# One quarter of a recurrent step as bf16 matmuls on three-part operands: the parts made on GpSimd, their rows summed on VectorE

## The chip, the cores and the metric

The kernel runs on one core of one Trainium2 chip. The core's engines each have a queue of their own and meet through semaphores: TensorE (PE; its weight loads are listed as PEld), VectorE (DVE), ScalarE (ACT), GpSimd (POOL) and SyncE (SP, which issues the transfers here). SBUF is the working memory; PSUM takes the matmuls' results, in banks. The metric is the device time of one execution in microseconds (us), the median of some runs.

## What is computed

A gated recurrent network with 512 units runs over 512 time steps for a batch of 8, and its states are added to the input:

```
def step(h, x_t):
    fused = sigmoid(concat([x_t, h]) @ w_W + w_b)
    hidden_state, output_state = split(fused, 2)
    memory_state = x_t @ wx_W + wx_b + hidden_state * (h @ wh_W + wh_b)
    h_new = output_state * h + (1.0 - output_state) * tanh(memory_state)
    return h_new, h_new
out = x + states
```

Below, r is the sum behind `hidden_state`, z the sum behind `output_state`, and h (as a bank's column) the sum `h @ wh_W + wh_b`. All tensors are float32. The parts that hang on x alone can be computed ahead; the three products of the state with 512x512 weights cannot, since each step needs the state of the step before.

## The kernel before

**Layout.** The 512 units are split over 128 partitions and 4 chunks, and the chunks into half A (chunks 0 and 1) and half B (2 and 3). For a step, PE multiplies the state (the stationary operand, 128 rows by 32 columns, of which only the 8 columns of this step are not zero) with weights (the moving operand). The output goes to four column tiles j of 32 partitions each. Four steps make a group: each has its own 8 of the 32 rows in a bank, so one bank serves four steps, and the x part of the sums is put there ahead.

**Banks of a step.** Bank A (192 columns, weights `wa`) holds h, z and r of half A; bank B (128 columns of `wb`) r and h of half B; and bank C, 64 columns of the PSUM tile `cs` (the other 64 of `wb`), z of half B. `ORDER` (line 26) is the order of a step on PE: `A0 B0 A1 A2 A3 B1 B2 B3 C0 C1 C2 C3`, where the digit is the chunk k of the state that is multiplied. A0, B0 and A1 need only half A of the new state, A2 is the first to need half B. Each entry is four matmuls (one for each j). A float32 matmul shows as two weight loads and two matmuls in the trace.

**Work on x.** Behind C3 stand the matmuls of `x_step` (lines 528-538), which prepare the x part of later groups. `SHARE` (line 48) deals them out: 384 columns a step in the first four steps of eight, 288 in the last four. There are none in steps 0 to 4, less towards the end, and none in the last five steps.

**Behind the matmuls.** Once bank A is done, DVE transposes r, h and z of half A (`turn_r`, `turn_h`, `turn_z`), so that units stand on partitions; ACT takes the sigmoids; DVE's scan `memory(hf, q)` forms the argument of tanh, ACT the tanh, and the scan `update(hf, q)` the new state, for one chunk q of half hf at a time. In DVE's queue half B's transposes stand around the first update of half A, then come half B's `memory` and `update` scans. ACT copies the new state to another slot, then does the group work: copies into banks (`spread`) and the moves of x sums. POOL adds the states to x for the output (`add`), two additions a step, and makes four x sums in eight steps (`x_sum`).

**Order.** All instructions are recorded in the order of the program and emitted engine by engine; `Flow.plan` (lines 132-214) finds the waits from what each instruction reads and writes. In PSUM any access to a bank waits for the latest access of any other engine to it. The emitting code has one line for all instructions, so every row of the profile reads L227; rows are told apart by their tiles.

Of the kernel before, what the change touches and what calls it, by code (L numbers as in the profile page):

```python
# [18 lines left out]
B = 8  # L19
# [3 lines left out]

DVE_FILL = 23
IDLE = 3
# [3 lines left out]

BANKS = {"A": 192, "B": 128, "C": 64}  # L30

# [55 lines left out]
class Flow:  # L87
# [44 lines left out]
    def plan(self):  # L132
# [9 lines left out]
        for i, item in enumerate(self.items):  # L142
# [71 lines left out]
            done.append(snap)  # L214

    def emit(self, tc):

# [21 lines left out]
def tile_cond_rnn_residual(  # L239
# [115 lines left out]
    NH = 2 * GS  # L355
    hT = [[pair(n, f"hT{n}{i}", 32, 3) for i in range(NH)] for n in "AB"]

# [13 lines left out]
    nc.scalar.activation(const.tile([P, 1], F32, name="table"), zeros[:, :1], AF.Sigmoid)  # L371
    for n, t_ in enumerate(hd0[0] + hd0[1] + md0[0] + md0[1] + hT[0] + hT[1]):
        (nc.vector if n < DVE_FILL else nc.gpsimd).memset(t_, 0.0)
    for t_ in hd0[0] + hd0[1]:
        nc.gpsimd.memset(t_[:, :, :, 1], -1.0)
# [10 lines left out]
    def state(hf, i, slot=2):  # L386
# [7 lines left out]
        {"A": wide[q]["A"][:, : BANKS["A"]],  # L394
         "B": wide[q]["B"][:, : BANKS["B"]],
         "C": cs[:, HU * q : HU * q + HU]}
        for q in range(2)
    ]
    xps = [psum.tile([P, 512], F32, name=f"xp{q}") for q in range(2)]
    piece = psum.tile([P, 512], F32, name="eps")  # L400
    eps = piece[HI, :W]

    def mm(out_, lhsT, rhs, start=False):
# [44 lines left out]
    def spread(g, names):  # L448

        for n in names:  # L450
            nc.scalar.copy(banks[g % 2][n], source(g)[:, XP[n]])

    def turn_x(g, hf):
# [101 lines left out]
    keep(0)  # L555
    spread(0, "ABC")
    for hf in range(2):
# [7 lines left out]
    for i in range(T):  # L565
# [8 lines left out]
        for n in (ORDER if i else FIRST).split():  # L574
            if n == "x":
                take(first[3], 1)
                continue
            bank, k = n[0], int(n[1])
            hs = hT[k // 2][i % NH][:, :, k % 2, 2]
            for j in range(NQ):  # L580
                mm(ps[bank][32 * j : 32 * j + 32, :], hs, wh(bank, k, j))
        if T - 17 <= i < T - 5:
# [6 lines left out]
        def scan(c_, out_, d0, d1):  # L589
# [10 lines left out]
            "h": (pa[:, :HU], ps["B"][:, HU:]),  # L600
            "z": (pa[:, HU : 2 * HU], ps["C"]),
            "r": (pa[:, 2 * HU :], ps["B"][:, :HU]),
# [25 lines left out]
        def turn_z(hf):  # L628
            tz, _ = turned("z", hf)
            if hf == 0:  # L630
# [32 lines left out]
        turn_h(1)  # L663
        update(0, 0)
        turn_z(1)
        nc.after(update(0, 1), r_done[1])
        if i == T - 1:
# [5 lines left out]
            )  # L673
        memory(1, 0)
        memory(1, 1)
        update(1, 0)
        update(1, 1)
        for hf in range(2):
            act(state(hf, i + 1, 0), state(hf, i + 1), AF.Copy)
        if i < 3:  # L680
            inst = load_x(i + 1)
            if i == 0:
                nc.after(inst, r_done[1])
# [6 lines left out]
        if o == LAST:  # L690
            if u == 2:
                spread(2 * o + 1, "AB")
                turn_x(2 * o + 1, 0)
                turn_x(2 * o + 1, 1)
            elif u == 3:
                spread(2 * o + 1, "C")
        elif u == 0:
            if o == 0:
                spread(1, "A")
            if sums:  # L700
                nc.scalar.copy(reg(BE), reg(AL))
# [4 lines left out]
        elif u == 1:  # L706
            if sums:
                nc.scalar.copy(more[HI], eps)
            spread(2 * o + 1, "BC" if o == 0 else "AC")
        elif u == 2:  # L710
# [3 lines left out]
            if o:  # L714
                spread(2 * o + 1, "B")
        elif u == 3:
            if sums:
# [132 lines left out]
```

## Time and profile before

| | us |
|---|---|
| median of 3 runs (lowest, highest) | 1654.64 (1654.48, 1655.43) |
| the profiled execution | 1657.46 |
| its span in the trace | 1655.7 |
| granted TensorE clock, mean | 0.999 |
| POOL busy | 301.9 |
| transfers, mean rate | 19 GB/s |

The span runs from the first to the last instruction of the program; 1.8 us of the profiled execution lie outside of it. A row of groups gives engine, operation, tiles (out<-in, without buffer numbers), shapes and count, then the busy time in us, the mean of one in ns, and the idle time of the engine before them with what ended it. A row of the timeline gives the start in us, how long the (merged) instructions took together in us, engine, line, operation, tiles, shapes and count; the brackets hold idle time before it and who ended that. Ends of matmuls are modelled, and include the way through the array, so that the distance of two starts says more than a duration.

### The profile page before, as it was taken

The numbers are of one execution on the slowest core, as the hardware profiler recorded it, in microseconds if no ns is written. First come the engines' busy times: TensorE is split into PE (matmuls) and PEld (weight loads), VectorE is DVE, ScalarE is ACT, GpSimd is POOL, SyncE is SP. The second block draws the span as 40 slices with busy tenths as digits, with TensorE's granted clock in tenths as the row PEclk, the third lists the DMA queues.
The fourth block names the chain that finished last, engine by engine and source line by source line (L and its number), as shares of the span: only waits on it lengthen the run. The fifth ranks groups of instructions, "written<-read, shape, count | busy, mean of one in ns | idle before, by whom it ended". The sixth has DMA issues, their size and how long they took to land.

```text
span 1655.7 us, 125580 instructions
## 1 busy us (share of the span) xinstructions
PE 1645.6 (99%) x54298; PEld 1500.2 (91%) x54298; DVE 1153.9 (70%) x9194; ACT 1193.8 (72%) x5998; POOL 301.9 (18%) x1279
## 2 busy tenths in 40 slices
PE   9999999999999999999999999999999999999998
PEld 5999999999999999999999999999999999999987
DVE  6776676676766766767667767677676766766765
ACT  3777777777777777777777777777777777777775
POOL 1211111111111111111111111111111111111111
PEclk9999999999999999999999999999999999999999
DMA  4000000000000000000000000000000000000000
GB/s 182 11 18 14 15 15 16 16 14 15 16 15 15 14 16 16 14 14 15 16 15 14 14 17 14 15 14 17 14 14 15 17 14 14 15 17 10 10 10 10
DMA packets 37284, 31.14 MB, mean 19 GB/s; under 512 B 4084, under 2 KB 35060, under 8 KB 36600
## 3 DMA queue, kind: packets, MB, share of 16 engines
q1 hardware_dynamic: 36576, 22.89, 4.5%
q8 instruction: 424, 6.95, 1.7%
q14 instruction: 132, 1.08, 0.2%
q10 hardware_dynamic: 152, 0.22, 0.1%
HBM read 14.70 MB, written 8.39 MB: 14 GB/s over the span
## 4 chain that ended last, share of the span: by engine, by line
PE 99%; DVE 1%; issue 0%; ACT 0%; DVEq 0%; SPq 0%
PE A L227 40%; PE B L227 26%; PE xp L227 18%; PE cs L227 13%; PE eps L227 1%; DVE tr L227 0%; DVE m L227 0%; DVE tz L227 0%; DVE md1B L227 0%; DVE md1A L227 0%; DVE hTA L227 0%; DVE hTB L227 0%; ACT hTB L227 0%; DVE zeros L227 0%; DVE rows L227 0%
## 5 line engine op out<-in xcount | busy, mean ns | idle before, releaser
L227 PE MATMUL A<-wa,hTA 128*32 128x192 f32 x8192 | 559.5, 326 | 2.4 <-DVE hTA L227 2.2
L227 PE MATMUL B<-wb,hTA 128*32 128x128 f32 x8192 | 454.8, 273 | 0.0
L227 PE MATMUL A<-wa,hTB 128*32 128x192 f32 x8192 | 448.6, 326 | 0.0
L227 PEld LDWEIGHTS A<-wa,hTA 128*32 128x32 f32 x8192 | 292.5, 122 | 124.6 <-DVE hTA L227 101.7
L227 DVE STREAM_TRANSPOSE tr<-A 128x64 f32<-128x64 f32 x512 | 128.0, 250 | 367.6 <-PE A L227 367.6
L227 POOL TENSOR_TENSOR ot<-xin,hTB 128x16 f32<-128x16 f32 x495 | 123.8, 250 | 1290.4 <-DVE hTB L227 1290.4
L227 PEld LDWEIGHTS B<-wb,hTA 128*32 128x32 f32 x8192 | 352.6, 122 | 2.8 <-issue 0.3
L227 PE MATMUL B<-wb,hTB 128*32 128x128 f32 x8192 | 339.6, 273 | 0.0
L227 PEld LDWEIGHTS A<-wa,hTB 128*32 128x32 f32 x8192 | 330.4, 122 | 9.1 <-DVE hTB L227 0.2
L227 ACT ACTIVATE md0A<-tr 128x16 f32<-128x16 f32 x512 | 112.4, 219 | 238.5 <-DVE tr L227 238.4
L227 PE MATMUL xp<-tw,sx 128*32 128x384 f32 (+2 forms) x1464 | 269.7, 433 | 0.0
L227 PEld LDWEIGHTS B<-wb,hTB 128*32 128x32 f32 x8192 | 262.3, 122 | 0.2 <-issue 0.2
L227 PE MATMUL cs<-wb,hTB 128*32 128x64 f32 x8192 | 230.3, 219 | 0.4 <-issue 0.3
L227 PE MATMUL cs<-wb,hTA 128*32 128x64 f32 x8192 | 230.2, 219 | 0.0
L227 DVE TENSOR_TENSOR_SCAN hTB<-hd0B,hTB 128x24 f32<-128x24 f32 x1024 | 158.0, 196 | 99.8 <-ACT hTB L227 99.8
L227 PE MATMUL xp<-wx,xin 128*32 128x384 f32 (+4 forms) x1348 | 219.1, 413 | 0.0
L227 PEld LDWEIGHTS cs<-wb,hTA 128*32 128x32 f32 x8192 | 207.5, 122 | 0.0
L227 DVE TENSOR_TENSOR_SCAN hTA<-hd0A,hTA 128x24 f32<-128x24 f32 x1024 | 190.9, 186 | 0.0
L227 ACT ACTIVATE hd0B<-tz 128x16 f32<-128x16 f32 x512 | 115.6, 226 | 94.5 <-DVE tz L227 94.5
L227 PEld LDWEIGHTS cs<-wb,hTB 128*32 128x32 f32 x8192 | 180.2, 122 | 0.7 <-issue 0.7
L227 ACT ACTIVATE hTB<-hTB 128x16 f32<-128x16 f32 x512 | 120.3, 235 | 79.1 <-DVE hTB L227 72.8
L227 ACT ACTIVATE hTA<-m 128x8 f32<-128x8 f32 x1024 | 160.8, 206 | 0.6 <-DVE m L227 0.3
(101 smaller groups left out, 2680.6 us busy)
## 6 DMA issues: line engine op xcount, KB each, us to landing
out_dram<-ot SPq DMA_DIRECT2D x128, 64.0 KB, 1.6
xin<-in_x_dram SPq DMA_DIRECT2D x112, 64.0 KB, 2.4
wx<-in_wx_dram SPq DMA_DIRECT2D x4, 768.0 KB, 7.0
wa<-in_wa_dram SPq DMA_DIRECT2D x4, 384.0 KB, 9.8
wb<-in_wb_dram SPq DMA_DIRECT2D x1, 1152.0 KB, 13.7
xin<-in_x_dram SPq DMA_DIRECT2D x3, 256.0 KB, 3.7
wb<-in_wb_dram SPq DMA_DIRECT2D x1, 384.0 KB, 14.1
head<-in_xh_dram ACTq DMA_DIRECT2D x1, 208.0 KB, 4.7
```

What stands on the lines that cost most here:

```text
L227: inst = getattr(self, item.op, getattr(engine, item.op, None))(*item.args, **item.kw)
```

## The change

z of half B (bank C) is no longer multiplied in float32. From step 3 on, h and the weights of bank C are each split into three bf16 parts that add up to the float32 number. The three parts of the 8 batch columns stand side by side as one stationary operand of 24 columns (`split`), loaded once for each k and j; three bf16 matmuls of 64 columns follow, one for each part of the weights (`wb` itself, of which the upper halves are read at every second bf16 element, `w2` and `w3`). The second and third are `kept`: they use the loaded operand again and have no weight load. Steps 0 to 2 stay float32.

- PE: an entry of C has 4 weight loads and 12 matmuls in place of 8 and 8.
- POOL makes the parts: two instructions for each half of the state, four in each step, ahead of the two additions; `w2` and `w3` once, at the end of step 0.
- The three parts come out in three groups of 8 rows, so the 32 rows of `cs` no longer serve four steps: each step has its own 64 columns, eight steps fill the tile. The x part is put into each step's columns by an ACT instruction with a mask (`spread_c`), zero but in 8 of the 32 rows: eight such instructions in eight steps in place of two copies.
- DVE sums the four groups of rows with a `tensor_reduce` behind the transpose. In half B the order on DVE becomes transpose, `memory(1, 0)`, the sum, `update(0, 1)`, `memory(1, 1)`, and on ACT the first tanh of half B comes ahead of the sigmoid of z.
- The states lie in one tile of both halves per ring place (`hs`, shown as hT), twice as wide as the data, the upper half zero. The start's fills are dealt out anew between DVE and POOL.

```diff
-DVE_FILL = 23
+DVE_FILL = 14
...
-BANKS = {"A": 192, "B": 128, "C": 64}
+BANKS = {"A": 192, "B": 128}
+PLAIN = 3
...
+    def kept(self, out, lhsT, rhs):
+        t = self.nc.tensor
+        return t.add_instruction(
+            mybir.InstMatmult(
+                name=self.nc.get_next_instruction_name(),
+                ins=[t.lower_ap(rhs), t.lower_ap(lhsT)],
+                outs=[t.lower_ap(out)],
+                start_tensor_calc=False,
+                stop_tensor_calc=False,
+                tile_size=(128, 32),
+                tile_position=(0, out.offset // 512 // 32 * 32),
+                bass_skip_group_check=True,
+                ldweights=False,
+                engine=mybir.EngineType.PE,
+            )
+        )
...
-    hT = [[pair(n, f"hT{n}{i}", 32, 3) for i in range(NH)] for n in "AB"]
+    hs = [const.tile([P, NQ, 64, 3], F32, name=f"hT{i}") for i in range(NH)]
+    hT = [[t_[:, 2 * n : 2 * n + 2, :32].rearrange("p c n s -> p n c s") for t_ in hs] for n in range(2)]
+    split = [const.tile([P, NQ, 3, B], F32, name=f"split{i}") for i in range(2)]
+    w2 = const.tile([P, NQ, NQ, HU], F32, name="w2")
+    w3 = const.tile([P, NQ, NQ, HU], F32, name="w3")
+    mask = const.tile([P, GS, 32], F32, name="mask")
...
-    for n, t_ in enumerate(hd0[0] + hd0[1] + md0[0] + md0[1] + hT[0] + hT[1]):
+    for n, t_ in enumerate(hd0[0] + hd0[1] + md0[0] + md0[1] + hs):
         (nc.vector if n < DVE_FILL else nc.gpsimd).memset(t_, 0.0)
+    steps = const.tile([P, GS, 32], F32, name="steps")
+    nc.vector.memset(steps, 0.0)
+    for n in range(GS):
+        nc.vector.memset(steps[:, n, B * n : B * n + B], 1.0)
+    nc.vector.transpose(mask.rearrange("p s n -> p (s n)"), steps.rearrange("p s n -> p (s n)"))
...
+    def high(t_):
+        return t_.bitcast(BF16)
+    def parts(out_, i, k, j):
+        lhsT = high(split[i % 2])[:, k].rearrange("p u b -> p (u b)")[:, 1::2]
+        for n, t_ in enumerate((wb[:, k, j, :HU], w2[:, k, j], w3[:, k, j])):
+            (nc.tensor.kept if n else mm)(out_, lhsT, high(t_)[:, 1::2])
...
+    def cell(i):
+        return cs[:, HU * (i % NH) : HU * (i % NH) + HU]
+
+    def spread_c(g, steps_):
+
+        for s in steps_:
+            nc.scalar.activation(
+                cell(GS * g + s), source(g)[:, XP["C"]], AF.Copy, scale=mask[:, s, :1]
+            )
...
-            hs = hT[k // 2][i % NH][:, :, k % 2, 2]
+            lhsT = hs[i % NH][:, k, :32, 2]
             for j in range(NQ):
-                mm(ps[bank][32 * j : 32 * j + 32, :], hs, wh(bank, k, j))
+                if bank == "C" and i >= PLAIN:
+                    parts(cell(i)[32 * j : 32 * j + 24], i, k, j)
+                else:
+                    to = cell(i) if bank == "C" else ps[bank]
+                    mm(to[32 * j : 32 * j + 32, :], lhsT, wh(bank, k, j))
...
-            tz, _ = turned("z", hf)
+            if hf:
+                t_, tz = tzb, tz_sum
+                nc.vector.tensor_reduce(
+                    tz, t_.rearrange("p c (u b) -> p c b u", u=4), mybir.AxisListType.X, ALU.add
+                )
+            else:
+                tz, _ = turned("z", hf)
...
+        tzb = work.tile([P, 2, 32], F32, tag="tzB", name=f"tzB_{i}")
+        tz_sum = work.tile([P, 2, B], F32, tag="tzs", name=f"tzs_{i}")
+        nc.vector.transpose(tzb.rearrange("p c n -> p (c n)"), raw["z"][1])
+        memory(1, 0)
         turn_z(1)
-        nc.after(update(0, 1), r_done[1])
+        update(0, 1)
...
-        memory(1, 0)
         memory(1, 1)
...
+            if PLAIN <= i + 1 < T:
+                ks, s1 = slice(2 * hf, 2 * hf + 2), B * ((i + 1) % GS)
+                t_, new = split[(i + 1) % 2][:, ks], hs[(i + 1) % NH][:, ks]
+                nc.gpsimd.tensor_tensor(
+                    t_[:, :, :2].rearrange("p k u b -> p k b u"),
+                    new[:, :, s1 : s1 + B, 2].unsqueeze(3).broadcast_to([P, 2, B, 2]),
+                    high(new).rearrange("p k (u n) s -> p k n u s", u=2)[:, :, s1 : s1 + B, :, 5],
+                    ALU.subtract,
+                )
+                nc.gpsimd.tensor_tensor(t_[:, :, 2], t_[:, :, 0], high(t_)[:, :, 0, 1::2], ALU.subtract)
+        if i == 0:
+            for to, t_ in ((w2, wb[:, :, :, :HU]), (w3, w2)):
+                nc.gpsimd.tensor_tensor(to, t_, high(t_)[:, :, :, 1::2], ALU.subtract)
...
-                spread(2 * o + 1, "C")
+                spread_c(2 * o + 1, (0, 1))
+            elif u == 4:
+                spread_c(2 * o + 1, (2, 3))
+            elif u < 2:
+                spread_c(2 * o, (2 + u,))
...
+                spread_c(2 * o, (2,))
...
-            spread(2 * o + 1, "BC" if o == 0 else "AC")
+            spread(2 * o + 1, "B" if o == 0 else "A")
+            if o:
+                spread_c(2 * o, (3,))
+            spread_c(2 * o + 1, (1,) if o else (0, 1))
...
+            spread_c(2 * o + 1, (2, 3))
...
+            spread_c(2 * o + 2, (0,))
...
-            spread(2 * o + 2, "C")
+            spread_c(2 * o + 2, (1,))
+            if o + 1 < LAST:
+                spread_c(2 * o + 3, (0,))
```

How this stands on the engines is shown at three places, each in a step with x work in the middle of the program. On PE, before, the end of a step (A, B and cs are the banks, hTA and hTB the halves of the state, the xp rows are x work):

```order
L227 MATMUL A_118<-wa,hTB_76 32x192 x8
L227 MATMUL B_119<-wb,hTA_68 32x128 x4
L227 MATMUL B_119<-wb,hTB_76 32x128 x8
L227 MATMUL cs<-wb,hTA_68 32x64 x8
L227 MATMUL cs<-wb,hTB_76 32x64 x8
L227 MATMUL xp_122<-wx,xin_133 32x384 x2
```

And with the change, from the last of bank B to the third pair of k and j (w_77 and w_78 are `w2` and `w3`, split_75 the parts of the state):

```order
L247 MATMUL B_117<-wb,hT_67 32x128 x12
L247 MATMUL cs<-wb,split_75 24x64
L221 MATMUL cs<-w_77,split_75 24x64
L221 MATMUL cs<-w_78,split_75 24x64
L247 MATMUL cs<-wb,split_75 24x64
L221 MATMUL cs<-w_77,split_75 24x64
L221 MATMUL cs<-w_78,split_75 24x64
L247 MATMUL cs<-wb,split_75 24x64
```

The 16 float32 matmuls of C became 48 in bf16, three for each pair; what stands ahead and behind is as before.

On DVE, before, from half B's transposes of r and h to the end of a step (tr and md1B are these, hTA and hTB are `update`, m is `memory`, tz<-cs the transpose of z of half B; the scans are listed here as SCALAR_TENSOR_TENSOR):

```order
L227 STREAM_TRANSPOSE tr_1_138<-B_119 128x64
L227 STREAM_TRANSPOSE md1B_89<-B_119 128x64
L227 SCALAR_TENSOR_TENSOR hTA_69<-hd0A_92,hTA_68 128x24
L227 STREAM_TRANSPOSE tz_1_139<-cs 128x64
L227 SCALAR_TENSOR_TENSOR hTA_69<-hd0A_92,hTA_68 128x24
L227 SCALAR_TENSOR_TENSOR m_1_135<-md0B_85,md1B_89 128x16 x2
L227 SCALAR_TENSOR_TENSOR hTB_77<-hd0B_94,hTB_76 128x24 x2
```

With the change (tzB is the transpose, tzs the sum over the row groups):

```order
L247 STREAM_TRANSPOSE tr_1_137<-B_119 128x64
L247 STREAM_TRANSPOSE md1B_87<-B_119 128x64
L247 SCALAR_TENSOR_TENSOR hT_73<-hd0A_89,hT_72 128x24
L247 STREAM_TRANSPOSE tzB_138<-cs 128x64
L247 SCALAR_TENSOR_TENSOR m_1_134<-md0B_83,md1B_87 128x16
L247 TENSOR_REDUCE tzs_139<-tzB_138 128x16
L247 SCALAR_TENSOR_TENSOR hT_73<-hd0A_89,hT_72 128x24
L247 SCALAR_TENSOR_TENSOR m_1_134<-md0B_83,md1B_87 128x16
L247 SCALAR_TENSOR_TENSOR hT_73<-hd0B_91,hT_72 128x24 x2
```

The first `memory` scan of half B moved ahead of the second update of half A, and the sum came between them. The first update of half A stays where it was.

On POOL, before, two steps (ot are the output additions, sx an x sum):

```order
L227 TENSOR_TENSOR ot_156<-xin_140,hTB_79 128x8x2
L227 TENSOR_TENSOR ot_156<-xin_140,hTA_71 128x8x2
L227 TENSOR_TENSOR sx_105<-xin_147 128x64
L227 TENSOR_TENSOR ot_156<-xin_140,hTB_80 128x8x2
L227 TENSOR_TENSOR ot_156<-xin_140,hTA_72 128x8x2
```

With the change, one step:

```order
L247 TENSOR_TENSOR split_76<-hT_72 128x2x8x2
L247 TENSOR_TENSOR split_76<-split_76 128x2x8
L247 TENSOR_TENSOR split_76<-hT_72 128x2x8x2
L247 TENSOR_TENSOR split_76<-split_76 128x2x8
L247 TENSOR_TENSOR sx_103<-xin_148 128x64
L247 TENSOR_TENSOR ot_124<-xin_140,hT_72 128x8x2 x2
```

The first pair of splits is that of half A and waits for its second update alone; the second pair waits for half B, as the output additions behind it did before.

More of the change, by code (lines that the diff above doesn't have):

```diff
@@ L394, in tile_cond_rnn_residual @@
         {"A": wide[q]["A"][:, : BANKS["A"]],
-         "B": wide[q]["B"][:, : BANKS["B"]],
-         "C": cs[:, HU * q : HU * q + HU]}
+         "B": wide[q]["B"][:, : BANKS["B"]]}
         for q in range(2)
@@ L555, in tile_cond_rnn_residual @@
     keep(0)
-    spread(0, "ABC")
+    spread(0, "AB")
+    spread_c(0, range(GS))
     for hf in range(2):
@@ L600, in tile_cond_rnn_residual @@
             "h": (pa[:, :HU], ps["B"][:, HU:]),
-            "z": (pa[:, HU : 2 * HU], ps["C"]),
+            "z": (pa[:, HU : 2 * HU], cell(i)),
             "r": (pa[:, 2 * HU :], ps["B"][:, :HU]),
@@ L699, in tile_cond_rnn_residual @@
                 spread(1, "A")
+            else:
+                spread_c(2 * o, (2,))
             if sums:
```

## The prediction

> **What bounds the kernel now.** I read the page first, then the timeline of PE alone, for the distance from step to step.
>
> ```profile
> PE 1645.6 (99%) x54298; PEld 1500.2 (91%) x54298; DVE 1153.9 (70%) x9194; ACT 1193.8 (72%) x5998; POOL 301.9 (18%) x1279
> ...
> PE 99%; DVE 1%; issue 0%; ACT 0%; DVEq 0%; SPq 0%
> ```
>
> PE is busy throughout and makes up the chain that ended last. But ends of matmuls are modelled, so this alone doesn't say how far the recurrence is from binding. The first matmuls of five steps in the middle say more:
>
> ```profile
> 800.25 0.55 PE L227 MATMUL A<-wa,hTA 128*32 128x192 f32 x8
> ...
> 803.36 0.55 PE L227 MATMUL A<-wa,hTA 128*32 128x192 f32 x8
> ...
> 819.40 0.59 PE L227 MATMUL A<-wa,hTA 128*32 128x192 f32 x8
> ...
> 822.67 0.59 PE L227 MATMUL A<-wa,hTA 128*32 128x192 f32 x8
> ...
> 825.77 0.53 PE L227 MATMUL A<-wa,hTA 128*32 128x192 f32 x6
> ```
>
> A step with 288 columns of x work takes 3.11 us (800.25 to 803.36), one with 384 takes 3.27 (819.40 to 822.67), and eight take 25.52, 3.19 each. No brackets: PE doesn't wait. The last steps, without x work, do:
>
> ```profile
> 1641.65 0.55 PE L227 MATMUL A<-wa,hTA 128*32 128x192 f32 x8 [0.24 <-DVE hTA L227]
> ...
> 1644.73 0.55 PE L227 MATMUL A<-wa,hTA 128*32 128x192 f32 x8 [0.24 <-DVE hTA L227]
> ...
> 1647.81 0.55 PE L227 MATMUL A<-wa,hTA 128*32 128x192 f32 x8 [0.24 <-DVE hTA L227]
> ```
>
> Here PE has less to do and waits for half A of the state, and a step still takes 3.08 us. **That is the floor of half A's loop** (A0 to A3, transposes, sigmoid, two scans, tanh, A0 again), and bank C isn't in it. So four steps of eight stand 0.03 above the floor and four 0.19: whatever PE saves, the short ones can give 0.03.
>
> **What C costs on PE, and will.**
>
> ```profile
> 800.57 0.44 PE L227 MATMUL B<-wb,hTA 128*32 128x128 f32 x8
> ...
> 802.42 0.40 PE L227 MATMUL cs<-wb,hTA 128*32 128x64 f32 x15
> ...
> 802.87 0.25 PE L227 MATMUL xp<-tw,xin 128*32 128x96 f32 x1
> ```
>
> C runs from 802.42 to 802.87: 0.45 us for 32 matmuls on four column tiles, so 0.056 for one of 64 columns on its tile. A0 takes 0.32 (800.25 to 800.57) for two of 192 columns on each tile, 0.16 each. That makes 0.83 ns a column and about 2.5 ns fixed. For bf16 there are only rows of the start:
>
> ```profile
> L227 PE MATMUL xp<-zeros 128*128 128x512 f32 x4 | 3.7, 1074 | 0.0
> ...
> L227 PE MATMUL cs<-none 128*128 128x512 bf16 x1 | 0.6, 610 | 2.3 <-DVE none L227 2.3
> ```
>
> Of the same width in the same stretch, the bf16 one took 610 ns and the float32 one 1074. So I take half of 0.83 a column: 64 columns make 0.027 + 0.0025 = 0.029, and twelve on each tile 0.35. **C saves 0.10 a step.** The other end is the float32 pace, 12 x 0.056 = 0.67, or 0.22 more than now. The operands are read at every second bf16 element, and a tile has three matmuls queued behind one load, which no row shows; half the time is the nearer, as it is the only bf16 row. The halved weight loads count as nothing, being hidden behind matmuls.
>
> The Trainium skill speaks against this edit: "TensorE: Matmul & The Clock Gate", section "Wait — 56ns, not 53.3ns?", says that matmuls never start closer than about 25 ns, however few their columns. For the engine as a whole, 48 matmuls would then take 1.2 us (an estimate from that page). The trace disagrees: 32 of them start in 0.45, 14 ns apart.
>
> **Half B's chain.** This is what the change lengthens, and its place in the step is a matter of 0.1 us:
>
> ```profile
> 799.93 0.21 DVE L227 TENSOR_TENSOR_SCAN hTA<-hd0A,hTA 128x24 f32<-128x24 f32 x1
> 800.06 0.22 DVE L227 STREAM_TRANSPOSE tz<-cs 128x64 f32<-128x64 f32 x1
> 800.20 0.24 PEld L227 LDWEIGHTS A<-wa,hTA 128*32 128x32 f32 x8 [0.26 <-DVE hTA L227]
> 800.21 0.17 DVE L227 TENSOR_TENSOR_SCAN hTA<-hd0A,hTA 128x24 f32<-128x24 f32 x1
> 800.29 0.25 DVE L227 TENSOR_TENSOR_SCAN m<-md0B,md1B 128x16 f32<-128x16 f32 x2
> 800.32 0.23 ACT L227 ACTIVATE hd0B<-tz 128x16 f32<-128x16 f32 x1 [0.18 <-DVE tz L227]
> 800.49 0.31 ACT L227 ACTIVATE hTB<-m 128x8 f32<-128x8 f32 x2
> 800.74 0.31 DVE L227 TENSOR_TENSOR_SCAN hTB<-hd0B,hTB 128x24 f32<-128x24 f32 x2 [0.20 <-ACT hTB L227]
> 801.12 0.88 PE L227 MATMUL A<-wa,hTB 128*32 128x192 f32 x16
> ```
>
> I count from 799.93, the first update of half A. The first update of half B starts at 0.81 and ends near 1.01 (0.20); A2 starts at 1.19. How late could it have been? A0's load started 0.06 after half A's state (800.14 to 800.20), its matmul 0.05 later, so 0.11: the state had to be there at 1.08, and **half B has 0.07 to spare** in a short step.
>
> Now the change. The transpose still follows the first update (0.13 to 0.35), however much earlier C is done, since DVE is busy until then. `memory(1, 0)` comes at 0.28. The sum needs the transpose: 0.41, if an instruction's wait costs the 0.06 above. For its price:
>
> ```profile
> L227 DVE MEMSET idle<- 128x1 f32 x1536 | 64.2, 59 | 6.7
> ...
> L227 DVE STREAM_TRANSPOSE md1A<-odd 128x64 f32<-128x64 f32 x63 | 14.1, 224 | 0.0
> ...
> L227 DVE TENSOR_TENSOR odd<-xp,both 64x384 f32<-64x384 f32 x61 | 33.6, 551 | 1.9
> ```
>
> It lies between 0.06 and 0.55; nearest is the transpose of as many elements from SBUF, so 0.22. It ends at 0.63, the sigmoid starts at 0.66 (ACT followed the transpose by 0.03 before, too), ends at 0.89, and the update may start at 0.92, 0.11 later than before. The tanh isn't late: its scan is earlier. The second update of half A moves from 0.28 to about 0.55 and ends at 0.72; A1, at 0.86 (the matmuls of A0 and B0 behind 800.25), needs it at 0.75. This is covered by 0.03.
>
> **The read port.** The first split follows that second update. POOL's rows, and two stretches of the start where it met DVE's scans:
>
> ```profile
> 1648.35 0.31 DVE L227 TENSOR_TENSOR_SCAN hTB<-hd0B,hTB 128x24 f32<-128x24 f32 x2 [0.19 <-ACT hTB L227]
> 1648.74 0.25 POOL L227 TENSOR_TENSOR ot<-xin,hTB 128x16 f32<-128x16 f32 x1 [2.63 <-DVE hTB L227]
> ...
> L227 POOL TENSOR_TENSOR sx<-xin 128x64 f32<-128x64 f32 x122 | 39.4, 323 | 0.0
> ...
> 29.97 1.02 POOL L227 TENSOR_TENSOR stepbias<-bias,stepbias 64x384 f32<-64x384 f32 x1 [3.26 <-ACT stepbias L227]
> 30.52 0.59 DVE L227 TENSOR_TENSOR_SCAN m<-md0A,md1A 128x16 f32<-128x16 f32 x2
> 31.26 0.24 POOL L227 TENSOR_TENSOR ot<-head,hTA 128x16 f32<-128x16 f32 x1
> 31.32 0.24 DVE L227 TENSOR_TENSOR_SCAN hTA<-hd0A,hTA 128x24 f32<-128x24 f32 x1
> ```
>
> A pair of scans took 0.59 beside a long POOL instruction, against 0.25 at 800.29, and a scan begun inside a short one ended 0.06 after it, 0.03 late. So POOL and DVE exclude each other, and a scan that loses ends 0.06 after POOL. POOL starts 0.08 behind a scan (1648.66 to 1648.74), so the split starts at 0.80. Between 0.25 for 16 elements and 0.32 for 64, its 32 cost 0.28, up to 0.40 if the strided bf16 reads are slow. It ends at 1.08, the scan at 1.14 instead of 1.12. Against 1.08 the state is 0.06 late; with 0.02 for weight loads that are then no longer ahead (part of the 0.05 from A0's load to its matmul) I take 0.08. A long step stays 0.09 above the floor (0.19 less the 0.10 that C saves), its A2 comes as much later, and that covers it.
>
> "SBUF — State Buffer" of the Trainium skill, section "Who interferes with whom", has the rule: a VectorE instruction with two SBUF inputs and a GpSimd one that reads SBUF share a port, held for the whole instruction. The 0.59 agrees; the 0.03 is less than a whole instruction.
>
> **Edits that I cost at nothing.** The splits of half B (ready by 1.9) are wanted at C2, behind 2.4. ACT gets six more instructions of 64 columns in eight steps:
>
> ```profile
> L227 ACT COPY cs<-even 128x64 f32<-128x64 f32 x63 | 13.2, 209 | 0.0
> ...
> L227 ACT ACTIVATE md0A<-tr 128x16 f32<-128x16 f32 x512 | 112.4, 219 | 238.5 <-DVE tr L227 238.4
> ```
>
> At most two in a step, 0.42, where ACT idles 238.5 / 512 = 0.47 on the mean ahead of half A's sigmoid; without that cover the rest would go onto the floor of those steps. Both waits of C for these writes are met before C begins.
>
> **Once.** `w2` and `w3` are 1024 columns each on POOL; by the 1.02 for 384 that is 2.7 each, in steps 1 and 2, where they block scans: between 0 and 5.4 us, I take 2. About twenty steps without full x work stand on the floor and get the 0.08 of half B: 1.6.
>
> **Sum.** In eight steps: four long ones save 0.10 each, less 0.01 where the first x matmul waits for its load: 0.36; four short ones 0.03: 0.12; four stalls of half B cost 0.32. That leaves 0.16 for eight steps, 0.02 a step; 486 such steps save 9.7. With 2 and 1.6 back, 6.1. The profiled execution is 1657.5, so 1651.4; the median lies 2.8 lower: **1648.5**, call it 1648.
>
> **Rivals.**
> - *Half B hidden*: the sum costs 0.14 or less and the split doesn't meet the scan. Then the stalls go: 0.48 for eight steps, 0.06 a step, 29 less 2: 1628. For it: the transpose's price includes work that a sum needn't do. Against: the port's rows.
> - *Half B's loop becomes the bound* (the slower one). Place: `update(1, 0)` behind sum and split. With a sum of 0.24 and a split of 0.34, the second update of half A ends at 0.74, the split runs from 0.82 to 1.16, and the scan ends at 1.22: 0.14 late in short steps, 0.05 in long ones (the 0.09). 4 x 0.14 + 4 x 0.05 - 0.48 = 0.28, or 0.035 a step, +17 + 5: 1677. With 0.28 and 0.40 it is 0.24 late, and the same sum gives +66 + 7: 1728. It decides from 0.105 late on, where the stalls eat the 0.48. For it: strided bf16 inputs, which no POOL row has. Against: both prices lie above the nearest rows.
> - *The port is held to the end of the split*: the scan then starts at 1.08 and ends at 1.28, 0.20 late: 4 x 0.20 + 4 x 0.11 - 0.48 = 0.76, +46 + 6: 1707. The Trainium skill's section above words it so. Against it stands the row of 0.24 at 31.32, where the scan ended 0.06 after POOL and not 0.20.
> - *The matmuls don't run at half price*: at float32's pace C costs 0.22 more in 509 steps, +112: 1767; if three on one tile hold up the next tile's, C takes 16 x 0.029 = 0.47 and with the stalls nearly nothing is gained: about 1668. For it: no row of such an operand.
> - *Nothing to be seen*: the terms cancel, 1655. Each is of the size of its error.
>
> **How the numbers follow.** Forecast (1640 to 1656) 0.45, half B hidden 0.13, half B's loop as bound 0.17, port held to the end 0.05, matmuls at more than half price 0.15 (half of it at the full price), cancelled 0.05. A measurement tells 0.2%, 3.3 us, from no change, so faster is below 1651.3: seven tenths of the forecast and the hidden case, 0.44; the same: the rest of the forecast and part of the cancelled, 0.17; slower 0.39. The range goes from the hidden case, 1628, past the loop's 1677 and the 1668 to 1705; the full-price matmuls, the port held to the end and the dearest sums, some 0.15 together, stay out.
>
> **What would show it.** Right: starts of cs and xp 0.35 apart; steps with 384 columns at 3.17 to 3.18; short ones at 3.08 and in those idle PE ahead of A2 released by DVE's scan of half B; the sum near 0.22; the first update of half B 0.1 later after that of half A. Wrong: cs to xp at 0.45 or more; ACT late at half A's sigmoid; a split over 0.35; no wait for half B at all.

## The result and the profile after

| | before | after |
|---|---|---|
| median of 4 runs, us | 1654.9 | 1727.7 |
| lowest and highest | 1654.5 to 1655.4 | 1725.3 to 1731.7 |
| span of the profiled execution | 1655.7 | 1723.4 |
| ratio, with its 95% interval | 1 | 1.0442 (1.0422 to 1.0463) |

The change makes the kernel 4.4% slower, 72.9 us; the forecast was 0.4% faster. The page of the changed kernel, engines and chain of waits first (time, instructions; then shares of the chain that ended last):

```profile
PE 1682.7 (98%) x62442; PEld 1313.6 (76%) x46154; DVE 1328.3 (77%) x9703; ACT 1331.9 (77%) x6382; POOL 770.7 (45%) x3318
...
PE 51%; ACT 26%; DVE 20%; issue 2%; DVEq 0%; SPq 0%
```

PE still looks busy all the time, as its modelled ends do. The chain says otherwise: PE made up 99% of it before, and now shares it with ACT and DVE. The groups that the prediction put prices on (operation, shapes, count, then total busy time and mean ns of one, then idle time ahead of them and what ended it):

```profile
L247 ACT ACTIVATE cs<-even,mask 128x64 f32<-128x64 f32 x252 | 77.6, 308 | 0.0
L247 ACT ACTIVATE cs<-odd,mask 128x64 f32<-128x64 f32 x252 | 72.3, 303 | 0.0
...
L247 ACT ACTIVATE md0A<-tr 128x16 f32<-128x16 f32 x512 | 110.0, 215 | 97.8 <-DVE tr L247 92.5
...
L247 DVE TENSOR_TENSOR_SCAN m<-md0A,md1A 128x16 f32<-128x16 f32 x1024 | 143.0, 182 | 57.1 <-ACT md0A L247 44.7
...
L247 DVE TENSOR_REDUCE tzs<-tzB 128x16 f32<-128x64 f32 x512 | 138.1, 270 | 0.5 <-DVE m L247 0.2
...
L247 POOL TENSOR_TENSOR split<-hT 128x32 f32<-128x32 f32 x1018 | 263.9, 259 | 845.5 <-DVE m L247 835.5
```

A masked write takes 0.30 us (the forecast used 0.21), the sum 0.27 (0.22), the first split 0.26 (0.28). ACT's idle time ahead of half A's sigmoid, 238.5 before, is down to 97.8, and DVE now waits 44.7 us for that sigmoid, where all its idle time ahead of these scans was 6.0 before. The first matmuls of four steps on PE, and in the second of them also the first of C and the first of the x work:

```profile
846.72 0.51 PE L247 MATMUL A<-wa,hT 128*32 128x192 f32 x8
...
849.91 0.55 PE L247 MATMUL A<-wa,hT 128*32 128x192 f32 x8
...
852.70 0.22 PE L247 MATMUL cs<-wb,split 128*24 128x64 bf16 x4 [0.31 <-ACT cs L247]
...
853.06 0.49 PE L247 MATMUL xp<-wx,xin 128*32 128x384 f32 x2
...
853.71 0.51 PE L247 MATMUL A<-wa,hT 128*32 128x192 f32 x8
...
857.26 0.57 PE L247 MATMUL A<-wa,hT 128*32 128x192 f32 x8
```

The three whole steps take 3.19, 3.80 and 3.55 us; before, each took 3.27. So the loss isn't spread evenly. Starts of A0 like these, for every step from 16 to 487, give the median distance for each place among the eight (0 to 3 have 384 columns of x work, 4 to 7 have 288), and the sum of eight; the rows below the second are experiments:

| us | 0 | 1 | 2 | 3 | 4 | 5 | 6 | 7 | eight |
|---|---|---|---|---|---|---|---|---|---|
| before | 3.27 | 3.27 | 3.27 | 3.27 | 3.11 | 3.11 | 3.11 | 3.11 | 25.49 |
| after | 3.43 | 3.18 | 3.79 | 3.49 | 3.04 | 3.16 | 3.18 | 3.17 | 26.45 |
| no masked writes | 3.30 | 3.18 | 3.18 | 3.18 | 3.05 | 3.16 | 3.18 | 3.17 | 25.40 |
| no sum | 3.22 | 3.18 | 3.47 | 3.28 | 3.04 | 3.08 | 3.10 | 3.08 | 25.44 |
| neither | 3.22 | 3.18 | 3.18 | 3.18 | 3.05 | 3.08 | 3.10 | 3.08 | 25.06 |
| B's copy last | 3.30 | 3.18 | 3.28 | 3.28 | 3.04 | 3.16 | 3.18 | 3.17 | 25.59 |
| masked writes alone | 3.27 | 3.27 | 3.39 | 3.27 | 3.11 | 3.11 | 3.11 | 3.11 | 25.62 |
| mixed, second | 3.18 | 3.20 | 3.19 | 3.18 | 3.11 | 3.11 | 3.11 | 3.11 | 25.18 |

Of the 0.96 us that eight steps lose, places 2 and 3 lose 0.75 and place 0 another 0.16. Fifty-nine such eights make 57 us of the 67.7 by which the span grew. The rest: the first sixteen steps, 5.8 longer (53.1 before, 58.9 now) though they begin 1.2 earlier; the last 24, 2.9 longer; and 3.6 in single steps that stretch (last section).

**What happens in place 2.** ACT alone, before and after, from the copy of half A's new state to the sigmoid of its z. First before, where the step's A0 started at 816.14:

```profile
816.86 0.23 ACT L227 ACTIVATE hTB<-hTB 128x16 f32<-128x16 f32 x1 [0.15 <-DVE hTB L227]
817.11 0.47 ACT L227 COPY more<-eps 64x384 f32<-64x384 f32 x1
817.59 0.32 ACT L227 COPY A<-odd 128x192 f32<-128x192 f32 x1
817.85 0.21 ACT L227 COPY cs<-odd 128x64 f32<-128x64 f32 x1
818.25 0.22 ACT L227 ACTIVATE md0A<-tr 128x16 f32<-128x16 f32 x1 [0.19 <-DVE tr L227]
```

Then after, where A0 started at 849.91:

```profile
851.01 0.24 ACT L247 ACTIVATE hT<-hT 128x16 f32<-128x16 f32 x1 [0.15 <-DVE hT L247]
851.26 0.47 ACT L247 COPY more<-eps 64x384 f32<-64x384 f32 x1
851.75 0.32 ACT L247 COPY A<-odd 128x192 f32<-128x192 f32 x1
852.01 0.31 ACT L247 ACTIVATE cs<-even,mask 128x64 f32<-128x64 f32 x1
852.26 0.30 ACT L247 ACTIVATE cs<-odd,mask 128x64 f32<-128x64 f32 x1
852.58 0.22 ACT L247 ACTIVATE md0A<-tr 128x16 f32<-128x16 f32 x1
```

Before, half A's sigmoid started 2.11 after A0 with 0.19 to spare. Now it starts 2.67 after A0, with nothing to spare. Two causes stand above each other in the list. The first line, ACT's copy of half B's state, came 0.72 after A0 and now comes at 1.10; everything below it in ACT's queue is moved by that 0.38. Half B's longer chain makes 0.23 of this: its second update ends 1.34 after the start of half A's first, where it was 1.11 (medians). The rest comes from A0, which here starts 0.26 after half A's first update, 0.42 before. Then two masked writes take the place of one plain one: 0.57 from the start of the first to the sigmoid, against 0.21 for the plain write, 0.36 more. Together that is 0.74 against 0.19 of room, so the sigmoid is 0.55 late, and half A's loop with it.

Two things follow from the late list. The first is a loop that closes without PE: when the sigmoid is late, DVE's scans of half A are late, then half B's scans behind them in DVE's queue, and then ACT's copy of half B's state, which heads the next list. In places 0, 1 and 3 ACT's idle time ahead of this sigmoid is now 0.00 (medians), so its list alone sets the sigmoid there. The second is C, which waits for ACT's last write. In places 0, 2 and 3 it starts 2.42, 2.79 and 2.49 after A0 (2.17 before), in every one of these steps 0.14 to 0.15 after the write has ended. The next A0 then starts 0.50, 0.40 and 0.50 after half A's first update, where 0.26 is enough in places 4 to 7. So PE comes 0.14 to 0.24 behind half A's state. Behind places 0 and 2 that costs nothing more, as ACT's list sets the next sigmoid anyway; behind place 3 it does, some 0.24 of the 0.96 (an estimate from these medians).

### The profile page after: what moved, and what is told of

Read it like the earlier page. It is cut to its first block, busy times and chain, and to the rows that moved or that the text cites. A ratio compares the mean times of both kernels' runs of the same rounds, so it can differ in the third digit from the quotient of the medians.

```text
span 1723.4 us, 129162 instructions
## 1 busy us (share of the span) xinstructions
PE 1682.7 (98%) x62442; PEld 1313.6 (76%) x46154; DVE 1328.3 (77%) x9703; ACT 1331.9 (77%) x6382; POOL 770.7 (45%) x3318
## 4 chain that ended last, share of the span: by engine, by line
PE 51%; ACT 26%; DVE 20%; issue 2%; DVEq 0%; SPq 0%
PE A L247 23%; PE B L247 12%; PE xp L247 9%; DVE hT L247 6%; ACT hT L247 6%; ACT cs L247 5%; DVE m L247 5%; PE cs L221 4%; ACT hd0B L247 3%; DVE tr L247 3%; PE cs L247 3%; ACT md0A L247 2%; DVE tzB L247 2%; DVE md1B L247 2%; ACT more L247 2%
## 5 line engine op out<-in xcount | busy, mean ns | idle before, releaser
L247 PE MATMUL A<-wa,hT 128*32 128x192 f32 x16384 | 901.3, 333 | 6.9 <-DVE hT L247 6.6
L247 PEld LDWEIGHTS A<-wa,hT 128*32 128x32 f32 x16384 | 496.5, 124 | 273.0 <-DVE hT L247 209.4
L247 PE MATMUL B<-wb,hT 128*32 128x128 f32 x16384 | 646.5, 273 | 0.2
L247 POOL TENSOR_TENSOR split<-hT 128x32 f32<-128x32 f32 x1018 | 263.9, 259 | 845.5 <-DVE m L247 835.5
L247 PEld LDWEIGHTS B<-wb,hT 128*32 128x32 f32 x16384 | 528.3, 122 | 33.9 <-DMA wb<-in_wb_dram 1.1
L247 ACT ACTIVATE hT<-m 128x8 f32<-128x8 f32 x2048 | 379.8, 210 | 167.2 <-DVE m L247 140.6
L247 ACT ACTIVATE hT<-hT 128x16 f32<-128x16 f32 x1024 | 230.9, 225 | 79.4 <-DVE hT L247 76.9
L247 PE MATMUL cs<-wb,split 128*24 128x64 bf16 x8144 | 254.8, 193 | 25.9 <-ACT cs L247 18.2
L221 PE MATMUL cs<-w,split 128*24 128x64 bf16 x16288 | 270.9, 192 | 0.1
L247 POOL TENSOR_TENSOR ot<-xin,hT 128x16 f32<-128x16 f32 x991 | 224.4, 250 | 1.6 <-DVE m L247 1.6
L247 DVE TENSOR_TENSOR_SCAN m<-md0A,md1A 128x16 f32<-128x16 f32 x1024 | 143.0, 182 | 57.1 <-ACT md0A L247 44.7
L247 ACT ACTIVATE md0A<-tr 128x16 f32<-128x16 f32 x512 | 110.0, 215 | 97.8 <-DVE tr L247 92.5
```

The lines of the kernel that those rows point to most:

```text
L221: return t.add_instruction(mybir.InstMatmult(name=self.nc.get_next_instruction_name(), ins=[t.lower_ap(rhs), t.lower_ap(lhsT)], outs=[t.lo ...
L247: inst = getattr(self, item.op, getattr(engine, item.op, None))(*item.args, **item.kw)
```

## The experiments

Each is the changed kernel with one edit, unless it says otherwise; times are of one execution each, beside 1656.8, 1656.6 and 1656.9 for the kernel before on the same chips. The first four ask which part the loss hangs on.

**No masked writes.**

```diff
-        for s in steps_:
+        for s in steps_ if g == 0 else ():
```

> Leaves out ACT's masked writes of x to bank C after the first group, so half B's z lacks its x part from the second group on; everything else stands. Two theories of the 73 us that the change lost. ACT theory: in the changed kernel the steps that carry two masked writes are the long ones (3.79 and 3.49 us, against 3.27 before), because these writes of 0.30 us delay C and half A's sigmoid. By it all steps with 384 columns of x come down to 3.18, the others stay at 3.04 to 3.18, and the time is 1645 to 1668. Half-B theory: the sum (0.27 us) and the scans beside GpSimd make the step, ACT only looks busy. By it the time stays above 1690.

Measured 1660.9, as the ACT theory has it. Places 1 to 3 come down to 3.18, and the short steps barely move; place 0 comes down from 3.43 to 3.30 only, which the theory didn't have. PE's starts in places 1 to 3, and then from 5 to 7:

```profile
842.82 0.50 PE L247 MATMUL A<-wa,hT 128*32 128x192 f32 x8
845.99 0.50 PE L247 MATMUL A<-wa,hT 128*32 128x192 f32 x8
849.17 0.51 PE L247 MATMUL A<-wa,hT 128*32 128x192 f32 x8
852.34 0.52 PE L247 MATMUL A<-wa,hT 128*32 128x192 f32 x8
...
855.39 0.55 PE L247 MATMUL A<-wa,hT 128*32 128x192 f32 x8
858.55 0.55 PE L247 MATMUL A<-wa,hT 128*32 128x192 f32 x8
861.74 0.55 PE L247 MATMUL A<-wa,hT 128*32 128x192 f32 x8
864.91 0.55 PE L247 MATMUL A<-wa,hT 128*32 128x192 f32 x8
```

Long steps of 3.17 to 3.18, short ones of 3.16 to 3.19: without ACT's writes these six are the steps of the forecast. The other two aren't. In places 0 and 5 to 7 C starts 2.30 after A0, in places 1 to 4 2.17 to 2.18 (medians); without the sum as well, the 2.30 is 2.21. So half B's stall falls on the four steps that follow a short one: place 0, a long one, doesn't cover it (3.30), and place 4, a short one behind a long one, has none (3.05).

**The same writes to a spare tile.**

```diff
-                cell(GS * g + s), source(g)[:, XP["C"]], AF.Copy, scale=mask[:, s, :1]
+                cell(GS * g + s) if g == 0 else spare, source(g)[:, XP["C"]], AF.Copy, scale=mask[:, s, :1]
```

> The same masked writes, at the same places in ACT's queue, but to a tile of SBUF that nobody reads (half B's z lacks its x part from the second group on). ACT is as busy as in the changed kernel, and C no longer waits for it. If the cost is C's wait, on the bank that ACT writes: 1650 to 1680, like the run without masked writes. If the cost is half A's sigmoid, late behind the writes: 1705 to 1720. If the masked writes don't matter (half-B theory): 1720 to 1730.

Measured 1744.3, above every expectation: with one spare tile each write waited for the one before and took 0.35 us, so ACT had more to do than in the changed kernel. The run was made again with eight tiles in turn.

> As the run with one spare tile (1744.3, where each write waited for the one before, 0.35 us each), but the masked writes go to eight spare tiles in turn, so they follow each other as closely as in the changed kernel; half B's z lacks its x part from the second group on. ACT's work stays, C's wait goes. If the late sigmoid of half A makes the loss: 1690 to 1730. If C's wait for the bank makes it: 1650 to 1685.

Measured 1717.9, within the expectation for the late sigmoid. C doesn't wait for ACT at all here, and only 9.8 of the 72.9 us come back. Half A's state now ends last, as at the end of this step in place 2 (3.65 long, 3.79 in the changed kernel):

```profile
847.48 0.55 PE L247 MATMUL A<-wa,hT 128*32 128x192 f32 x8
...
851.13 0.55 PE L247 MATMUL A<-wa,hT 128*32 128x192 f32 x8 [0.16 <-DVE hT L247]
```

The writes took 0.34 each, 0.04 more than in the changed kernel, so what C's wait costs by itself isn't known better than "the smaller part".

**No sum.**

```diff
-                t_, tz = tzb, tz_sum
-                nc.vector.tensor_reduce(
-                    tz, t_.rearrange("p c (u b) -> p c b u", u=4), mybir.AxisListType.X, ALU.add
-                )
+                tz = tzb[:, :, :B]
```

> Leaves out the sum of the four row groups: half B's sigmoid reads the first group of the transposed bank C alone. ACT theory: the steps with masked writes stay long, the sum is paid mainly in the steps without them, where 0.03 to 0.1 us each comes back: 1695 to 1715. Half-B theory: the update of half B is 0.2 us earlier in every step and the loss goes with it: 1675 or less.

Measured 1678.3 (18 us of it in single stretched steps), nearer to the half-B theory, although the writes were all there. In place 2 the step is 0.33 shorter, in place 3 0.21. So neither theory was right alone: 66.8 and 49.5 together exceed the loss, and the two must act through one another.

**No splits.**

```diff
-            if PLAIN <= i + 1 < T:
+            if PLAIN <= i + 1 < PLAIN + 2:
```

> GpSimd makes the parts of h only for steps 3 and 4; later steps multiply by these old parts, so half B's z is that of an old state. It takes away 1018 pairs of GpSimd instructions, so the scans of half B never meet a split. If that meeting costs what the prediction took (a scan 0.02 to 0.06 us late in the steps that wait for half B): 1700 to 1717. If it is covered: 1722 to 1730.

Measured 1717.6, between the two ranges and 10.1 less; by the medians of the steps it is 0.12 in eight, or 7 us: places 0 and 2 are 0.08 to 0.09 shorter, place 1 is 0.08 longer, the short steps gain up to 0.01 each. DVE's scans of half B in this run, and in the changed kernel:

```profile
L247 DVE TENSOR_TENSOR_SCAN hT<-hd0B,hT 128x24 f32<-128x24 f32 x1024 | 200.7, 208 | 49.0
```

```profile
L247 DVE TENSOR_TENSOR_SCAN hT<-hd0B,hT 128x24 f32<-128x24 f32 x1024 | 200.8, 212 | 48.8
```

So meeting a split costs little. Half B's first scan overlaps with one in every step from 16 to 487 of the changed kernel and takes 216 ns there, 208 here (medians); the second takes 208 in both. Where the 0.08 of places 0 and 2 comes from, no run shows.

**Half B's copy last.** If the sum acts on the writes through the head of ACT's queue, it should be enough to move that head.

```diff
-            act(state(hf, i + 1, 0), state(hf, i + 1), AF.Copy)
+            if hf == 0:
+                act(state(hf, i + 1, 0), state(hf, i + 1), AF.Copy)
...
+        act(state(1, i + 1, 0), state(1, i + 1), AF.Copy)
```

> The runs so far: without masked writes 1660.9 (66.8 less than the changed kernel), without the sum 1678.3 (49.5 less); together more than the 72.9 lost, so the two aren't added up. Theory of the queue: ACT takes the masked writes behind its copy of half B's new state, which waits for half B's update; the sum makes that update later, so the writes both start later and last longer, and the sigmoid of half A behind them pays for both. This run moves only the copy of half B's state to the end of the step's list, behind the masked writes. By the theory of the queue the steps with two writes lose most of their excess: 1665 to 1690. Rival: it is ACT's sum of work in these steps, whatever its order: 1715 to 1730.

Measured 1685.0: one instruction moved, and 42.7 us of 72.9 are back. By the medians it is 0.86 of the 1.05 that taking all masked writes away gives; the time shows less because 16 us of this execution lie in single stretched steps. ACT's rows in place 2 (A0 at 830.95):

```profile
831.54 0.22 ACT L247 ACTIVATE hT<-hT 128x16 f32<-128x16 f32 x1
831.77 0.47 ACT L247 COPY more<-eps 64x384 f32<-64x384 f32 x1
832.25 0.32 ACT L247 COPY A<-odd 128x192 f32<-128x192 f32 x1
832.51 0.31 ACT L247 ACTIVATE cs<-even,mask 128x64 f32<-128x64 f32 x1
832.76 0.30 ACT L247 ACTIVATE cs<-odd,mask 128x64 f32<-128x64 f32 x1
833.08 0.23 ACT L247 ACTIVATE hT<-hT 128x16 f32<-128x16 f32 x1
833.21 0.20 ACT L247 ACTIVATE md0A<-tr 128x16 f32<-128x16 f32 x1
```

The list now starts 0.82 after A0 instead of 1.35, and the sigmoid 2.26 after it instead of 2.67.

**Masked writes alone.** Bank C in float32, no parts of the state and no sum, DVE's order of before. The cells and their masked writes remain, and `w2` and `w3` are still made at the start.

```diff
-                if bank == "C" and i >= PLAIN:
+                if bank == "C" and bf(i):
...
-            if hf:
+            if hf and bf(i):
...
-        nc.vector.transpose(tzb.rearrange("p c n -> p (c n)"), raw["z"][1])
-        memory(1, 0)
+        if bf(i):
+            nc.vector.transpose(tzb.rearrange("p c n -> p (c n)"), raw["z"][1])
+            memory(1, 0)
         turn_z(1)
-        update(0, 1)
+        up = update(0, 1)
+        if not bf(i):
+            nc.after(up, r_done[1])
...
+        if not bf(i):
+            memory(1, 0)
...
-            if PLAIN <= i + 1 < T:
+            if i + 1 < T and bf(i + 1):
```

(`bf(i)` is false in every step.)

> The masked writes at the places of the change, but bank C with float32 matmuls, no parts, no sum, and VectorE's order as before the change. By the theory of the queue the writes alone cost little, since half B's copy comes early again: 1658 to 1672. If the writes cost the 66.8 us by themselves, 1700 or more.

Measured 1671.3. Place 2 alone is longer, by 0.12: with half B's copy early, two writes miss their room by little. That is 7.4 us of the 14.7 lost; another 6.4 is the start, 59.5 for the first sixteen steps against 53.1, though no parts of the state are made in them.

**Plain copies.**

```diff
-            nc.scalar.activation(
-                cell(GS * g + s), source(g)[:, XP["C"]], AF.Copy, scale=mask[:, s, :1]
-            )
+            nc.scalar.copy(cell(GS * g + s), source(g)[:, XP["C"]])
```

> The same writes at the same places, as plain copies without the mask (the sum then adds x of four steps instead of one), which took 0.21 us each before the change where a masked one takes 0.30. It prices the step of the prediction that used 0.21. By the theory of the queue two writes at 0.21 still miss their gap behind the later copy of half B: 1680 to 1705. If the mask's price alone had made the loss: 1660 to 1670.

Measured 1704.3. At the price that the forecast used (0.21) the kernel would still have lost 47 us; the wrong price explains 23, or 30 by the medians of the steps (25.94 for eight).

**Neither writes nor sum.** The edits of "no masked writes" and "no sum" together.

> Leaves out the masked writes after the first group and the sum of the row groups (half B's z is then neither complete nor summed). If the two losses simply added up (66.8 and 49.5), this would be 1611. By the theory of the queue the sum costs 49.5 only because ACT's late writes multiply it; without them it costs what half B's own loop is longer, about 0.1 us in the four short steps and the step after them: 1632 to 1650. It is also the change's PE saving with nearly nothing against it.

Measured 1640.3. Without the writes the sum is worth 20.6 (1660.9 to 1640.3), with them 49.5. By the medians, which leave single stretched steps out, it is 20 and 60; and the writes are worth 22 without the sum and 62 with it.

**Masked writes by DVE.** One instruction writes the cells of four steps, in places 1 and 6; ACT writes only those of the first group and of the last two.

```diff
-        for s in steps_:
+        for s in steps_ if g == 0 or g // 2 == LAST else ():
...
+        nc.vector.tensor_tensor(
+            cs[:, q : q + HU * GS].rearrange("p (s n) -> p s n", s=GS),
+            source(g)[:, XP["C"]].unsqueeze(1).broadcast_to([P, GS, HU]),
+            mask[:, :, :1].broadcast_to([P, GS, HU]),
+            ALU.mult,
+        )
```

> The masked writes of a group of four steps made by one VectorE instruction of 256 columns (state times mask, the mask broadcast), in steps 1 and 6 of eight, where VectorE has no sums to make; ACT has none left. Both theories: as without masked writes, 1655 to 1668, if VectorE does 256 columns in about 0.4 us (384 took 0.55) inside the 0.8 us that it has between half B's update and the next transposes. If it is late there: up to 1685.

Measured 1663.5, within 3 us of the run without masked writes. So the change can be had for 64 us less, and is still 0.4% slower than before, in one execution: half B's longer chain leaves 0.10 in eight steps (25.39) of what C saves, 6 us, and the first sixteen steps alone cost 6.6 (59.7 against 53.1).

**A mixed kernel.** That chain does no harm where PE sets the pace. So bf16 parts and sum only in the long steps, float32 in the short ones.

```diff
+    def bf(i):
+        return i >= PLAIN and i % NH in SPLIT
```

(`SPLIT` is `(0, 1, 2, 3)`; the tests of the run "masked writes alone" follow it, and DVE writes the masked cells.)

> A version meant to beat both kernels: the bf16 matmuls, the parts and the sum only in the four steps of eight with 384 columns of x, where PE sets the pace; the other four keep float32 matmuls and no sum. Masked writes only for those four steps, by one VectorE instruction; the other four share one plain write by ACT. By the steps seen: long ones 3.18 (3.27 before), short ones 3.11 as before: 8 steps save 0.34 us, 61 times, 21 us, less 4 to 7 at the start: 1638 to 1646. If a wait for half B behind the sum reaches the short steps, or the long ones: 1650 to 1665.

Measured 1653.5, median of 5, ratio to before 0.9968 (0.9954 to 0.9982). The steps came out as expected (3.18 to 3.19, and 3.11), the gain didn't: 12 us lie in single stretched steps, and the first sixteen steps are 4.1 longer. The second can be mended.

```diff
-PLAIN = 3
+PLAIN = 16
...
-        if i == 0:
-            for to, t_ in ((w2, wb[:, :, :, :HU]), (w3, w2)):
-                nc.gpsimd.tensor_tensor(to, t_, high(t_)[:, :, :, 1::2], ALU.subtract)
+        if 8 <= i < 16:
+            ks = slice(i % 4, i % 4 + 1)
+            to, t_ = ((w2, wb[:, :, :, :HU]), (w3, w2))[i // 12]
+            inst = nc.gpsimd.tensor_tensor(to[:, ks], t_[:, ks], high(t_)[:, ks, :, 1::2], ALU.subtract)
+            nc.after(inst.ins, done)
```

> The mixed kernel (1653.5, ratio 0.9968) with a cheaper start: float32 in bank C for the first 16 steps, w2 and w3 made in eight pieces in steps 8 to 15 behind half B's update, the mask made in step 9. The first 16 steps took 57.2 us there and 53.1 before the change; with 53.3 it gains about 4 us: 1645 to 1651. If the single stretched steps (64 steps, 12 us in the profile, in which PE waits for nothing the profile names) are more frequent: up to 1656.

Measured 1648.0, median of 5 (1645.8 to 1648.8), ratio 0.9943 (0.9930 to 0.9957): it beats both kernels, the one before by 0.6% and the changed one by some 80 us.

## Why the prediction was wrong, step by step

- **C's saving: right.** "C saves 0.10 a step." In the changed kernel C starts at 803.18 and x follows at 803.53:

```profile
803.18 0.22 PE L247 MATMUL cs<-wb,split 128*24 128x64 bf16 x4
...
803.53 0.49 PE L247 MATMUL xp<-tw,sx 128*32 128x384 f32 x1
```

  That is 0.35, the value taken. The rule of the Trainium skill that was weighed there ("TensorE: Matmul & The Clock Gate", section "Wait — 56ns, not 53.3ns?") doesn't hold here for the engine as a whole: 48 of them on four column tiles in 0.35 us are 7 ns apart. On one tile they are 29 ns apart, twelve in 0.35, which stays above the 25. Long steps at 3.17 to 3.18 are there too, in places 1 to 3 without the masked writes.
- **Half B's chain: nearly right, for the part that was worked out.** The sum takes 0.27 and not 0.22, and the first update of half B starts 0.94 after that of half A (median; 0.92 forecast, 0.80 before). What the step left out is the second update. Its tanh follows a scan that is now behind half A's second update, so the pair takes longer, and ends 1.34 after half A's first update instead of 1.11:

```profile
850.59 0.39 DVE L247 TENSOR_TENSOR_SCAN hT<-hd0B,hT 128x24 f32<-128x24 f32 x2
```

  It was 0.31 before. ACT's copy of half B's state waits for the pair, and that copy is the head of the list in which the masked writes stand.
- **The read port: small, as forecast, and smaller still.** The scan was to end 0.02 later beside the split (1.14 and not 1.12); it takes 8 ns more. It ends 0.05 to 0.07 after the split in every step, as the 0.06 has it, but without a split it would end nearly there as well, so this doesn't test the port. With the dearer sum, which starts the scan later, places 5 to 7 came out at 3.16 to 3.18 all the same, where 3.08 and a stall of 0.08 make 3.16. If the rule of "SBUF — State Buffer" in the Trainium skill, section "Who interferes with whom", is read as holding the port for the whole instruction, a scan would have to wait for the end of the split. The trace disagrees: the scan starts 0.10 after the split's start and takes 0.22, and the split takes 0.26 (medians).
- **"Edits that I cost at nothing": this is the step that failed.** Its words were that ACT's additional writes, "0.42, where ACT idles 238.5 / 512 = 0.47 on the mean", are covered. Three things were wrong with it. The price came from the plain copy (0.209), and the masked write takes 0.30: 23 to 30 us, by the run with plain copies. (The Trainium skill has this price: "ScalarE: Activation LUTs", section "What ACT_TABLE_LOAD costs", adds about 93 ns for each scale or bias that is read from a pointer for each partition; the rows here show 94 to 99, 303 and 308 against 209.) The room was a mean over all steps; the places with two writes had 0.40 (place 0), 0.19 (2) and 0.51 (3) ahead of the sigmoid before (medians), and the 0.19 stood in the timeline. And the room was taken as fixed, while the same change delayed the head of the list by 0.38 in place 2. The last is shown by the run that moves only that copy, and by the writes' price beside the sum, 66.8, and without it, 38.0 (1678.3 to 1640.3; the first of these two executions has 18 us in single stretched steps, and by the medians the price is 62 beside the sum and 22 without it).
- **"Both waits of C for these writes are met before C begins": wrong in places 0, 2 and 3,** where C starts 0.14 to 0.15 after ACT's last write (the row with 0.31 at 852.70 is one of them). It is the smaller part: taking the wait away brought back 9.8 us, with writes that were 0.04 dearer.
- **Once: too small.** 2 and 1.6 us were put down; the first sixteen steps take 5.8 more. The second mixed kernel's cheaper start (53.2) shows that it is avoidable.
- **The sum.** Without the masked writes, eight steps take 25.40, 0.09 less than before; the forecast had 0.16 less. The terms for PE and half B were thus 4 us off in all, but partly by luck: place 0 came out 0.13 longer than a long step of the forecast, and place 4 0.11 shorter than a short one. None of the rivals was what happened: they asked about half B, the port and the matmuls. The 1728 in one of them is the measured time by chance: it stands on a split of 0.40, which took 0.26, and a stall of half B in every step, and that chain without the masked writes gives 1660.9. ACT stood only under what would show the forecast wrong ("ACT late at half A's sigmoid"), without a time or a chance.

## What to carry to other kernels

An engine's mean idle time ahead of an instruction is no cover: read the gap in the very step that gets the additional work, and then ask what heads the engine's queue there and whether the same change makes that later. Two delays that each nearly fit into the room can meet in one in-order queue; each then costs about three times what it costs without the other (62 and 22, 60 and 20 us here), and taking either away seems to cure most of the loss. Where a change trades PE time for latency, use it only in the steps in which PE sets the pace.

## What was not expected of the hardware

- ACT's masked write of 128x64 took 0.30 us to PSUM, and 0.34 to SBUF in the run with eight tiles.
- One VectorE product of 256 columns with both inputs broadcast took 0.40 to 0.43 us, less than two of ACT's masked writes of 64:

```profile
L247 DVE TENSOR_TENSOR cs<-odd,mask 128x256 f32<-128x256 f32 x63 | 27.1, 430 | 0.0
L247 DVE TENSOR_TENSOR cs<-even,mask 128x256 f32<-128x256 f32 x62 | 24.8, 401 | 0.0
```

- Single steps stretch: they take 0.04 to 0.9 us more than the median of their place, and not always in the same place. From step 8 to 494 it was 10 steps with 1.5 us together before, 50 with 7.3 after, 49 with 11 in the second mixed kernel, 86 with 19 without the sum. PE then waits in the middle of a bank for nothing that the profile names, as here in the first mixed kernel (weight loads of PE):

```profile
614.43 0.10 PEld L249 LDWEIGHTS cs<-wb,split 128*24 128x24 bf16 x2 [0.55 <-issue]
```

  All nine such stalls of 0.18 us or more inside C in that execution, and all twelve in that of the second mixed kernel, ended 1.3 to 1.5 us after the last packet of the larger instruction queue, taken to be PE's, had arrived (424 packets of 16 KB, one every 3.9 us on the mean). So instruction supply is suspected, but no run tested it. These steps alone can set two single executions 15 us apart; that is why the table goes by medians.
